# An LSTM with a residual: first loads, first products and the activation table rearranged

## The chip, the cores and the metric

The kernel runs on one core of a Trainium2 chip. A time is the device time of one execution in microseconds (us); where several are given, their median counts. A profile describes one execution; its span runs from the first to the last instruction. The engines are named as the profile names them: PE (TensorE, with PEld for its weight loads), DVE (VectorE), ACT (ScalarE), POOL (GpSimd) and SP (SyncE, which issues all DMAs here).

## The reference, cut to what matters

x is 32 sequences of 512 steps with 512 features, in float32. One LSTM layer of width 512 runs over the steps, and its output is added to x:

```
xW = einsum('ntd,dg->ntg', x, Wx) + b          # Wx: 512 x 2048
a = xW[:, t] + h @ Wh                          # Wh: 512 x 2048
i, f, o = sigmoid(a[:, :3*512]);  g = tanh(a[:, 3*512:])
c = f * c + i * g;   h = o * tanh(c)
x + h of all steps
```

The products with Wx are free of the recurrence; those with Wh are not: step t+1 needs h of step t.

## The kernel before, in words

Four gates of 512 values for 32 sequences are held as a tile of 128 partitions (4 blocks j of 32 sequences' rows) by 4 gates by 128, exactly one PSUM bank. TensorE is used as four column strips of 32: every product is issued for j = 0 to 3 in turn, each j writes 32 partitions of the bank, and the profile shows each product as two MATMUL records (128 x 32 weights loaded by PEld, then 128 or 512 moving columns).

Per step t there are three kinds of work.

- `h_part(t)`: 16 products of 512 columns, h of step t-1 times Wh (L427 in the profile). They add to the bank `gates_of(t)`: `ge` for even t, `go[0]` and `go[1]` in turn for odd t.
- `cell(t)`: ACT's sigmoids and tanh, DVE's products and the two transposes that give `ht`, which the next `h_part` waits for (L440 to L459). The residual add is POOL's, the output DMA SP's.
- The products with Wx. For four steps together (a "quad") they are made by a two-level Strassen-Winograd scheme: sums of x (`early_sums`, `late_sums`), sums of weights (`outer_weight`, `inner_weight`, made once by DVE) and 128-column products (`inner`, L314) whose results are combined over several steps. It has a pipeline 11 steps long (`LEAD`). So the first eight steps and the last eight, for which it has no room, are made by plain products: `direct` (L341) multiplies a chunk of x by the raw Wx blocks. For one step, `direct` with `ALL` goes over four pairs (k, gg), each with e, g and j: 64 products of 128 columns, one gate each.

The order of the work is written out by hand in the loop over k at the end (`manual_schedule`): window k holds `h_part(k - 11)`, `evacuate(k)`, the biases of `bias_at`, sums, `make_weights(k)`, `input_part(k)`, the plain products of `direct_at` and `cell(k - 11)`. Every engine executes its part of that list in order. The start is windows 8, 9 and 10, where there is no `h_part` yet: there the plain products of steps 0, 1 and 3 are made as pieces of Wx arrive, four pairs over three windows; those of step 2 (whose bank `ge` is still in use by step 0) come in window 12 behind `input_part`, followed by steps 5, 4, 7 and 6 in windows 13 to 16. A bank is emptied by `clear` (products of zeros with `start`, 16 of 128 columns) and given the bias by `set_bias`, an ACT copy.

All loads are issued on SP in program order: x chunks 0 and 1 (8 steps each, 512 KB), the bias, h0, four loads of Wx of 1 MB, four of Wh of 1 MB. They use eight DMA semaphores in turn, so a load is issued only when the load eight places ahead of it has landed. The Wx blocks lie in `w_sb[1]`, `w12`, `w_sb[2]` and `w_sb[3]`, slots 0 to 3 of each; in the host's layout the four blocks have the order (e, g) = (0,0), (1,0), (1,1), (0,1). In the tail, one block of each of two tiles has been overwritten by then and is loaded again by `reload` at window 505 (256 KB each).

Of the kernel before, what the change touches and what calls it, by code (L numbers as in the profile page):

```python
# [20 lines left out]
LAST = T // 4 - 2  # L21
# [7 lines left out]
def kernel(  # L29
# [59 lines left out]
    def gates_of(t):  # L89
        if t >= 4 * LAST:  # L90
            return last_banks[t - 4 * LAST]
        return ge if t % 2 == 0 else go[(t % 4) // 2]


    xcs, sums = {}, {}

    def load_chunk(c):
        xc = xpool.tile([P, TC, NJ, B], F32, name=f"xc_{c}", tag="xc")
        nc.sync.dma_start(out=xc.rearrange("p t q b -> p (t q b)"), in_=x[c])
        xcs[c] = xc  # L100
# [67 lines left out]

    load_chunk(0)
    load_chunk(1)
    bias_sb = const.tile([P, G, P], F32, name="bias_sb")
    for j in range(NJ):
        nc.sync.dma_start(
            out=bias_sb[j * B : (j + 1) * B, :, :],
            in_=bias[j].unsqueeze(0).to_broadcast([B, G, P]),
        )
    h_init = const.tile([P, NJ, B], F32, name="h_init")  # L180
    nc.sync.dma_start(out=h_init.rearrange("p q b -> p (q b)"), in_=h0)
    w_sb = {r: const.tile([P, 8 if r == 1 else 7, NJ, P], F32, name=f"w_{r}") for r in range(1, 8)}
    w12 = const.tile([P, 4, NJ, P], F32, name="w12")
    raw = {(0, 0): w_sb[1], (0, 1): w12, (1, 0): w_sb[2], (1, 1): w_sb[3]}
    for i in ((0, 0), (0, 1), (1, 0), (1, 1)):
        nc.sync.dma_start(out=raw[i][:, 0:4].rearrange("p s j u -> p (s j u)"), in_=wx[2 * i[0] + i[1]])
    wh_sb = const.tile([P, NJ, NJ, G * P], F32, name="wh_sb")
    for k in range(NJ):
        nc.sync.dma_start(out=wh_sb[:, k], in_=wh[:, k])

    def outer_weight(r):
        a, b = {5: (w12, w_sb[1]), 7: (w_sb[3], w12), 6: (w_sb[3], w_sb[5]), 4: (w_sb[2], w_sb[6])}[r]
        nc.vector.tensor_sub(w_sb[r][:, 0:4], a[:, 0:4], b[:, 0:4])

    def inner_weight(r, s):
        w = w_sb[r]
        a, b = {5: (3, 0), 6: (2, 4), 7: (2, 3), 4: (1, 5)}[s]
        nc.vector.tensor_sub(w[:, place(r, s)], w[:, a], w[:, b])

    def place(r, s):  # L200
        return 7 if (r, s) == (1, 4) else s - 1

    def raw_block(k, gg, e, g, late):
        n = {(0, 0): 0, (1, 0): 1, (1, 1): 2, (0, 1): 3}[e, g]
        if late and k == 1 and n == 3:
            return w_sb[5][:, 4 + gg]
        return raw[k, gg][:, n]

    def reload():

        for gg in range(2):
            nc.sync.dma_start(
                out=w_sb[5][:, 4 + gg].rearrange("p j u -> p (j u)"),
                in_=wx[2 + gg][:, 3 * NJ * P : 4 * NJ * P],
            )


# [2 lines left out]
    zero = const.tile([P, P], F32, name="zero")  # L220
# [5 lines left out]

    def clear(bank):

        for n in range(4):
            for j in range(NJ):  # L230
                nc.tensor.matmul(
                    bank[j * B : (j + 1) * B, n],
                    zero[:, 0:B],
                    zero,
                    start=n == 0,
                    stop=True,
                    skip_group_check=True,
                )

    U = {}  # L240

    def start_sums():
        nc.vector.tensor_sub(db, bias_sb[:, 2:4], b1)
        nc.vector.memset(xr1, 0.0)
        nc.vector.tensor_copy(xr1[:, 2], b1[:, 0])
        nc.vector.tensor_copy(xr5[:, 2], db[:, 0])
# [84 lines left out]
        for s in ss:  # L331
            inner(r, s, quad, dst[s])

    def direct(t, pairs):

        c, tt = divmod(t, TC)
        for k, gg in pairs:
            for e in range(2):
                for g in range(2):
                    for j in range(NJ):  # L340
                        nc.tensor.matmul(  # L341
                            gates_of(t)[j * B : (j + 1) * B, 2 * gg + g],
                            xcs[c][:, tt, 2 * k + e],
                            raw_block(k, gg, e, g, t >= 4 * LAST)[:, j],
                            start=False,
                            stop=True,
                            skip_group_check=True,
                        )

    def set_bias(t):  # L350
        nc.scalar.copy(gates_of(t), bias_sb)

    def quad_at(r, k, stage):

# [140 lines left out]
    def make_weights(k):  # L495
        for what in weights.get(k - 4 * FIRST, ()):
            outer_weight(what) if isinstance(what, int) else inner_weight(*what)


    ALL = ((0, 0), (0, 1), (1, 0), (1, 1))  # L500
    bias_at = {12: (2,), 13: (5,), 14: (4,), 15: (7,), 16: (6,)}
    direct_at = {
        8: [(t, ALL[0:1]) for t in (0, 1, 3)] + [(t, ALL[1:2]) for t in (0, 1, 3)],
        9: [(t, ALL[2:3]) for t in (0, 1, 3)],
        10: [(t, ALL[3:4]) for t in (0, 1, 3)],
        **{k: [(t[0], ALL)] for k, t in bias_at.items()},
    }
    end = 4 * LAST
    free_at = (510, 511, 510, 511, 513, 513, 514, 515)
    todo = [(end + i, (pair,)) for i in range(8) for pair in ALL]  # L510
# [13 lines left out]
    assert not todo  # L524

    with tc.manual_schedule():
        for bank in (ge, *go, pp):
            clear(bank)
        for t in (0, 1, 3):
            set_bias(t)  # L530
        for op in early_sums(nc.gpsimd, 1):
            op()
        start_sums()
        make_weights(4 * FIRST - 1)
        early, late = {}, {}
        for k in range(4 * FIRST, WINDOWS):
            t = k - LEAD
            c, rest = divmod(k + 5, TC)
            if rest == 0 and 2 <= c < NCHUNK:
                load_chunk(c)  # L540
            if k == 4 * LAST + 1:
                reload()
            if t >= 0:
                h_part(t)
            evacuate(k)
            for i in bias_at.get(k, ()):
                if gates_of(i) in (pb, *pa):
                    clear(gates_of(i))
                set_bias(i)
            for first, make, made, cut in ((-1, early_sums, early, 5), (3, late_sums, late, 3)):  # L550
                c, rest = divmod(k - first, TC)
                if (2 if make is early_sums else 1) <= c < NCHUNK - 1 and rest in (0, 2):
                    if rest == 0:
                        made[c] = make(nc.vector, c)
                    for op in made[c][:cut] if rest == 0 else made.pop(c)[cut:]:
                        op()
            make_weights(k)
            if t < 0:
                for what in direct_at.get(k, ()):
                    direct(*what)  # L560
            input_part(k)
            if t >= 0:
                for what in direct_at.get(k, ()):
                    direct(*what)
                cell(t)
# [5 lines left out]
def _laid_out(name, a):  # L571

    import numpy as _np

    if name == "x":
        a = a.reshape(B, NCHUNK, TC, NJ, NJ, B).transpose(1, 3, 5, 2, 4, 0).reshape(NCHUNK, P, TC * P)
    elif name == "cond_1024":
        a = a.reshape(B, NJ, NJ, B).transpose(1, 3, 2, 0).reshape(P, P)
    elif name == "L0_cond_Wx":

        a = a.reshape(NJ, 2, 2, B, 2, 2, NJ, P).transpose(1, 4, 0, 3, 2, 5, 6, 7).reshape(4, P, 4, NJ * P)
        a = a[:, :, [0, 2, 3, 1]].reshape(4, P, 4 * NJ * P)
    elif name == "L0_cond_Wh":
        a = a.reshape(NJ, NJ, B, G, NJ, P).transpose(0, 2, 1, 4, 3, 5).reshape(P, NJ, NJ, G * P)
    else:
        a = a.reshape(G, NJ, P).transpose(1, 0, 2)
    return _np.ascontiguousarray(a)
# [22 lines left out]
```

## Time and profile before

| what | value |
|---|---|
| median of three runs | 3177.79 us (3177.13 to 3181.36) |
| the profiled execution's own time | 3177.66 us |
| its span | 3175.6 us |
| PE busy | 3153.6 us, 99% |
| DVE, ACT, POOL busy | 70%, 40%, 8% |
| PE idle, 6.50 to 11.36 us | 4.86 us |
| PE idle, 19.32 to 20.72 and 24.41 to 26.90 us | 1.40 and 2.48 us |
| first `h_part` starts | 29.3 us |
| second `h_part` starts | 36.54 us |

The profile has a page and answers on parts of it. The chain of work lists, in order of time, what the last instruction was waiting for, step by step back to the start; "issue" in it is time for which the profile shows no cause. The timeline lists groups of instructions with start, duration, engine, line, written and read tiles, their shape and count, and in brackets the engine's idle time before them with what ended it. The windows view gives each engine's busy time in chosen stretches. In the DMA view q1 is the queue of the kernel's loads and stores and q8 a queue of instruction blocks.

### The profile page before, as it was taken

What the parts mean: (1) busy time and instruction counts of PE and PEld (TensorE: products, weight loads), DVE (VectorE), ACT (ScalarE), POOL (GpSimd) and SP (SyncE); (2) the same over time, 40 slices, a digit from 0 to 9 for tenths busy, and PEclk for the clock granted to TensorE, in tenths of its full rate; (3) what the DMA queues carried; (4) which work ended last, traced back from release to release, by engine and by line L of the source; (5) the groups of instructions that cost most, each with busy time, mean ns of one, the idle gap of its engine ahead of it and who ended that gap; (6) DMA issues with size and microseconds to landing.
All of it is one profiled execution on the core that took longest, in us unless ns stands there. A gap on an engine that the chain in (4) does not pass through costs nothing.

```text
span 3175.6 us, 151795 instructions
## 1 busy us (share of the span) xinstructions
PE 3153.6 (99%) x67296; PEld 1925.2 (61%) x67296; DVE 2232.2 (70%) x9226; ACT 1277.5 (40%) x4190; POOL 241.8 (8%) x525
## 2 busy tenths in 40 slices
PE   8999999999999999999999999999999999999999
PEld 6666666666666666666666666666666666666655
DVE  6777777777777777777777777777777777777762
ACT  2343444344434444444444444444444444444432
POOL 0000000000000000000000000000000000000000
PEclk9999999999999999999999999999999999999999
DMA  3000000000000000000000000000000000000000
GB/s 137 26 20 28 26 21 26 28 20 28 20 28 26 21 26 28 20 28 20 28 26 21 27 28 20 28 20 28 26 21 26 28 20 28 20 28 26 21 26 14
DMA packets 48659, 86.07 MB, mean 27 GB/s; under 512 B 5376, under 2 KB 38400, under 8 KB 46976
## 3 DMA queue, kind: packets, MB, share of 16 engines
q1 hardware_dynamic: 48000, 76.37, 7.5%
q8 instruction: 525, 8.60, 1.1%
q14 instruction: 134, 1.10, 0.1%
HBM read 42.80 MB, written 33.55 MB: 24 GB/s over the span
## 4 chain that ended last, share of the span: by engine, by line
PE 99%; DVE 1%; ACT 0%; DMA 0%; issue 0%; SPq 0%; DVEq 0%; ACTq 0%
PE go L427 27%; PE ge L427 27%; PE pa L314 18%; PE pp L314 10%; PE pb L314 6%; PE ge L314 5%; PE go L314 3%; PE go L341 1%; PE ge L341 1%; PE pa L427 0%; PE pa L341 0%; DMA w<-in_L_cond_Wx_dram 0%; PE pp L341 0%; ACT s L440 0%; PE pb L427 0%
## 5 line engine op out<-in xcount | busy, mean ns | idle before, releaser
L427 PE MATMUL go<-wh_sb,ht 128*32 128x512 f32 x8128 | 918.7, 592 | 5.9 <-DVE ht L459 5.8
L427 PE MATMUL ge<-wh_sb,ht 128*32 128x512 f32 x8064 | 911.4, 592 | 0.9 <-DVE ht L459 0.8
L449 DVE TENSOR_TENSOR fc<-s,c 128x128 f32<-128x128 f32 x511 | 149.5, 292 | 577.4 <-ACT s L440 577.4
L427 PEld LDWEIGHTS go<-wh_sb,ht 128*32 128x32 f32 x8128 | 255.4, 110 | 464.1 <-issue 454.7
L427 PEld LDWEIGHTS ge<-wh_sb,ht 128*32 128x32 f32 x8064 | 256.5, 110 | 454.0 <-issue 415.8
L470 POOL TENSOR_TENSOR oc<-xc,ht 128x128 f32<-128x128 f32 x511 | 237.2, 464 | 2919.3 <-issue 1467.9
L440 ACT ACTIVATE s<-ge 128x256 f32<-128x256 f32 x253 | 97.1, 384 | 823.1 <-PE ge L427 823.1
L314 PE MATMUL pa<-w,n 128*32 128x128 f32 x5952 | 299.2, 273 | 0.0
L455 ACT ACTIVATE ig<-c 128x64 f32<-128x64 f32 x1024 | 206.1, 248 | 220.9 <-DVE c L453 220.9
L440 ACT ACTIVATE s<-go 128x256 f32<-128x256 f32 x254 | 97.5, 384 | 439.9 <-PE go L427 439.9
L457 DVE TENSOR_TENSOR fc<-s,ig 128x64 f32<-128x64 f32 x1024 | 190.1, 226 | 97.3 <-ACT ig L455 97.3
L314 PEld LDWEIGHTS pa<-w,n 128*32 128x32 f32 x5952 | 180.9, 110 | 75.4 <-issue 38.6
L314 PEld LDWEIGHTS pa<-w,na 128*32 128x32 f32 x3968 | 124.3, 110 | 148.6 <-issue 110.4
L258 ACT COPY u<-pp 128x512 f32<-128x512 f32 x248 | 145.4, 586 | 141.4 <-PE pp L314 141.4
L314 PE MATMUL pa<-w,na 128*32 128x128 f32 x3968 | 199.6, 273 | 0.0
L314 PE MATMUL pa<-w,nb 128*32 128x128 f32 x3968 | 199.3, 273 | 0.0
L314 PE MATMUL pp<-w,sa 128*32 128x128 f32 x3968 | 199.3, 273 | 0.0
L459 DVE STREAM_TRANSPOSE ht<-fc 128x64 f32<-128x64 f32 x1024 | 190.6, 224 | 1.5 <-DVE fc L457 0.9
L451 DVE TENSOR_TENSOR ig<-s 128x64 f32<-128x64 f32 x1024 | 181.3, 219 | 0.0
L453 DVE TENSOR_TENSOR c<-fc,ig 128x64 f32<-128x64 f32 x1024 | 181.2, 219 | 0.0
L314 PEld LDWEIGHTS pa<-w,nb 128*32 128x32 f32 x3968 | 121.2, 110 | 74.2 <-issue 38.0
L369 DVE TENSOR_TENSOR p<-u,p 128x512 f32<-128x512 f32 x124 | 86.0, 694 | 113.9 <-ACT u L258 113.9
(148 smaller groups left out, 5326.6 us busy)
## 6 DMA issues: line engine op xcount, KB each, us to landing
xc<-in_x_dram SPq DMA_DIRECT2D x64, 512.0 KB, 3.9
out_dram<-oc SPq DMA_DIRECT2D x255, 128.0 KB, 2.0
w<-in_L_cond_Wx_dram SPq DMA_DIRECT2D x4, 1024.0 KB, 9.5
wh_sb<-in_L_cond_Wh_dram SPq DMA_DIRECT2D x4, 1024.0 KB, 17.1
w<-in_L_cond_Wx_dram SPq DMA_DIRECT2D x2, 256.0 KB, 4.1
bias_sb<-in_L_cond_b_dram SPq DMA_DIRECT2D x4, 64.0 KB, 4.6
h_init<-in_cond_dram SPq DMA_DIRECT2D x1, 64.0 KB, 4.0
out_dram<-oc SPq DMA_DIRECT2D x1, 64.0 KB, 1.6
```

Of the source, the lines that this page charges most:

```text
L258: nc.scalar.copy(u, pp)
L314: nc.tensor.matmul(dst[j * B : (j + 1) * B], operand(r, s, quad), w_sb[r][:, place(r, s), j], start=start, stop=True, skip_group_check=True,)
L369: nc.vector.tensor_add(U["p5", q], U[4, q], U["p5", q])
L427: nc.tensor.matmul(g[j * B : (j + 1) * B], state["ht"][:, k, :], wh_sb[:, k, j, :], start=False, stop=True, skip_group_check=True,)
L440: nc.scalar.activation(s[:, 0:2, :], g[:, 0:2, :], AF.Sigmoid)
L449: nc.vector.tensor_mul(fc, s[:, 1, :], state["c"])
L451: nc.vector.tensor_mul(ig[:, u], s[:, 0, u], s[:, 3, u])
L453: nc.vector.tensor_add(c[:, u], fc[:, u], ig[:, u])
L455: nc.scalar.activation(tc_t[:, u], c[:, u], AF.Tanh)
L457: nc.vector.tensor_mul(h[:, u], s[:, 2, u], tc_t[:, u])
L459: nc.vector.transpose(ht[:, 2 * i : 2 * i + 2].rearrange("p q b -> p (q b)"), h[:, u])
L470: nc.gpsimd.tensor_add(state["oc"][:, tt % 2], xcs[n][:, tt], ht)
```

## The change

- **Loads.** Chunk 0 of x comes in two halves; only the first (steps 0 to 3) is loaded first, the second after Wh. The bias is second. Each Wx load is split in two of 512 KB, in the order in which the products use them, and chunk 1 goes between the second and third pair of them. h0 goes after Wx.
- **Step 2.** In windows 8 to 10 the products of steps 2, 0 and 1 are made. Those of step 2 use the bank of step 3; when they are complete, `park` copies the bank (bias included) to SBUF, and `set_bias(2)` in window 12 copies it from there in place of the bias. Step 3's products follow: two pairs in window 10, one in window 11, one in window 12, the latter two behind `input_part`. Window 12 no longer has step 2's 64 products.
- **Width.** `direct` makes products of 256 columns (two gates), 32 for a step in place of 64. For that the Wx blocks lie in the order (e, g) = (0,0), (0,1), (1,0), (1,1), and the slots of sums (`place`, `inner_weight`) and the blocks reloaded in the tail follow (512 KB each).
- **Clear.** `clear` makes four products of 512 columns of zeros, in place of 16 of 128.
- **Table.** A sigmoid of the zero tile is ACT's first instruction. ACT then has one table load in the program, where it had one before its first copy and one before the first sigmoid.

```diff
+    load_first(0)
     for j in range(NJ):
         nc.sync.dma_start(out=bias_sb[j * B : (j + 1) * B, :, :], ...)
+    load_raw(0, 0)
+    load_raw(0, 1)
+    load_chunk(1)
+    load_raw(1, 0)
+    load_raw(1, 1)
     nc.sync.dma_start(out=h_init.rearrange("p q b -> p (q b)"), in_=h0)
-    for i in ((0, 0), (0, 1), (1, 0), (1, 1)):
-        nc.sync.dma_start(out=raw[i][:, 0:4].rearrange("p s j u -> p (s j u)"), in_=wx[2 * i[0] + i[1]])
     for k in range(NJ):
         nc.sync.dma_start(out=wh_sb[:, k], in_=wh[:, k])
+    load_first(1)
...
     def clear(bank):
-        for n in range(4):
-            for j in range(NJ):
-                nc.tensor.matmul(bank[j * B : (j + 1) * B, n], zero[:, 0:B], zero, start=n == 0, ...)
+        for j in range(NJ):
+            nc.tensor.matmul(
+                bank[j * B : (j + 1) * B], zero[:, 0:B],
+                zero.unsqueeze(1).to_broadcast([P, 4, P]), start=True, stop=True,
+            )
...
-    def direct(t, pairs):
+    def direct(t, pairs, bank=None):
         for k, gg in pairs:
             for e in range(2):
-                for g in range(2):
-                    for j in range(NJ):
-                        nc.tensor.matmul(
-                            gates_of(t)[j * B : (j + 1) * B, 2 * gg + g],
-                            xcs[c][:, tt, 2 * k + e],
-                            raw_block(k, gg, e, g, t >= 4 * LAST)[:, j], ...
+                for j in range(NJ):
+                    nc.tensor.matmul(
+                        bank[j * B : (j + 1) * B, 2 * gg : 2 * gg + 2],
+                        xcs[c][:, tt, 2 * k + e],
+                        raw_blocks(k, gg, e, t >= 4 * LAST)[:, :, j], ...
...
     def set_bias(t):
-        nc.scalar.copy(gates_of(t), bias_sb)
+        nc.scalar.copy(gates_of(t), parked.pop(t, bias_sb))
+    def park(t, bank):
+        parked[t] = upool.tile([P, 4, P], F32, name="parked", tag="u3")
+        nc.scalar.copy(parked[t], bank)
...
-    direct_at = {
-        8: [(t, ALL[0:1]) for t in (0, 1, 3)] + [(t, ALL[1:2]) for t in (0, 1, 3)],
-        9: [(t, ALL[2:3]) for t in (0, 1, 3)],
-        10: [(t, ALL[3:4]) for t in (0, 1, 3)],
-        **{k: [(t[0], ALL)] for k, t in bias_at.items()},
-    }
+    direct_at = {k: [(t, ALL) for t in bias_at[k] if t > 2] for k in bias_at}
+    direct_at[11], direct_at[12] = [(3, ALL[2:3])], [(3, ALL[3:4])]
+    def first_direct(k):
+        pairs = {8: ALL[0:2], 9: ALL[2:3], 10: ALL[3:4]}.get(k, ())
+        for pair in pairs:
+            direct(2, (pair,), gates_of(3))
+            if k == 10:
+                park(2, gates_of(3))
+                set_bias(3)
+            for t in (0, 1):
+                direct(t, (pair,))
+        if k == 10:
+            direct(3, ALL[0:2])
...
+        warm = work.tile([P, G, P], F32, name="warm", tag="s")
+        nc.scalar.activation(warm[:, 0], zero, AF.Sigmoid)
-        for bank in (ge, *go, pp):
+        for bank in (go[1], ge, go[0], pp):
             clear(bank)
-        for t in (0, 1, 3):
+        for t in (3, 0, 1):
             set_bias(t)
```

More of the change, by code (lines that the diff above doesn't have):

```diff
@@ L167, in operand, with load_first, load_raw @@
         return z["n" + group][:, SUM[s], 2 * i + d]
-    load_chunk(0)
-    load_chunk(1)
-    bias_sb = const.tile([P, G, P], F32, name="bias_sb")
+    xcs[0] = xpool.tile([P, TC, NJ, B], F32, name="xc_0", tag="xc")
+    def load_first(half):
+        n = TC // 2
+        nc.sync.dma_start(
+            out=xcs[0][:, half * n : (half + 1) * n].rearrange("p t q b -> p (t q b)"),
+            in_=x[0][:, half * n * P : (half + 1) * n * P],
+        )
+    bias_sb = const.tile([P, G, P], F32, name="bias_sb")
+    h_init = const.tile([P, NJ, B], F32, name="h_init")
+    w_sb = {r: const.tile([P, 8 if r == 1 else 7, NJ, P], F32, name=f"w_{r}") for r in range(1, 8)}
+    w12 = const.tile([P, 4, NJ, P], F32, name="w12")
+    raw = {(0, 0): w_sb[1], (0, 1): w12, (1, 0): w_sb[2], (1, 1): w_sb[3]}
+    wh_sb = const.tile([P, NJ, NJ, G * P], F32, name="wh_sb")
+    def load_raw(k, gg):
+        for e in range(2):
+            nc.sync.dma_start(
+                out=raw[k, gg][:, 2 * e : 2 * e + 2].rearrange("p s j u -> p (s j u)"),
+                in_=wx[2 * k + gg][:, 2 * e * NJ * P : 2 * (e + 1) * NJ * P],
+            )
+    load_first(0)
     for j in range(NJ):
@@ L179 @@
         )
-    h_init = const.tile([P, NJ, B], F32, name="h_init")
-    nc.sync.dma_start(out=h_init.rearrange("p q b -> p (q b)"), in_=h0)
-    w_sb = {r: const.tile([P, 8 if r == 1 else 7, NJ, P], F32, name=f"w_{r}") for r in range(1, 8)}
-    w12 = const.tile([P, 4, NJ, P], F32, name="w12")
-    raw = {(0, 0): w_sb[1], (0, 1): w12, (1, 0): w_sb[2], (1, 1): w_sb[3]}
-    for i in ((0, 0), (0, 1), (1, 0), (1, 1)):
-        nc.sync.dma_start(out=raw[i][:, 0:4].rearrange("p s j u -> p (s j u)"), in_=wx[2 * i[0] + i[1]])
-    wh_sb = const.tile([P, NJ, NJ, G * P], F32, name="wh_sb")
+    load_raw(0, 0)
[3 more added lines that the diff above has]
+    load_raw(1, 1)
+    nc.sync.dma_start(out=h_init.rearrange("p q b -> p (q b)"), in_=h0)
     for k in range(NJ):
         nc.sync.dma_start(out=wh_sb[:, k], in_=wh[:, k])
+    load_first(1)
     def outer_weight(r):
@@ L196, in inner_weight, with raw_blocks @@
         w = w_sb[r]
-        a, b = {5: (3, 0), 6: (2, 4), 7: (2, 3), 4: (1, 5)}[s]
+        a, b = {5: (1, 0), 6: (3, 4), 7: (3, 1), 4: (2, 5)}[s]
         nc.vector.tensor_sub(w[:, place(r, s)], w[:, a], w[:, b])
     def place(r, s):
[L201 to L207, printed above, removed]
+        return 7 if (r, s) == (1, 4) else {1: 0, 2: 2, 3: 3, 4: 1}.get(s, s - 1)
+    def raw_blocks(k, gg, e, late):
+        if late and k == 1 and e == 0:
+            return w_sb[5][:, 2 * gg : 2 * gg + 2]
+        return raw[k, gg][:, 2 * e : 2 * e + 2]
     def reload():
@@ L212, in reload @@
             nc.sync.dma_start(
-                out=w_sb[5][:, 4 + gg].rearrange("p j u -> p (j u)"),
-                in_=wx[2 + gg][:, 3 * NJ * P : 4 * NJ * P],
+                out=w_sb[5][:, 2 * gg : 2 * gg + 2].rearrange("p s j u -> p (s j u)"),
+                in_=wx[2 + gg][:, 0 : 2 * NJ * P],
             )
@@ L227, in clear @@
     def clear(bank):
-        for n in range(4):
-            for j in range(NJ):
-                nc.tensor.matmul(
[L232 to L238, printed above, removed]
+        for j in range(NJ):
+            nc.tensor.matmul(
+                bank[j * B : (j + 1) * B],
+                zero[:, 0:B],
+                zero.unsqueeze(1).to_broadcast([P, 4, P]),
+                start=True,
+                stop=True,
+            )
     U = {}
@@ L332, in private @@
             inner(r, s, quad, dst[s])
-    def direct(t, pairs):
+    def direct(t, pairs, bank=None):
         c, tt = divmod(t, TC)
+        bank = gates_of(t) if bank is None else bank
         for k, gg in pairs:
             for e in range(2):
-                for g in range(2):
-                    for j in range(NJ):
-                        nc.tensor.matmul(
-                            gates_of(t)[j * B : (j + 1) * B, 2 * gg + g],
-                            xcs[c][:, tt, 2 * k + e],
[L344 to L348, printed above, removed]
+                for j in range(NJ):
+                    nc.tensor.matmul(
+                        bank[j * B : (j + 1) * B, 2 * gg : 2 * gg + 2],
+                        xcs[c][:, tt, 2 * k + e],
+                        raw_blocks(k, gg, e, t >= 4 * LAST)[:, :, j],
+                        start=False,
+                        stop=True,
+                        skip_group_check=True,
+                    )
+    parked = {}
     def set_bias(t):
-        nc.scalar.copy(gates_of(t), bias_sb)
+        nc.scalar.copy(gates_of(t), parked.pop(t, bias_sb))
+    def park(t, bank):
+        parked[t] = upool.tile([P, 4, P], F32, name="parked", tag="u3")
+        nc.scalar.copy(parked[t], bank)
     def quad_at(r, k, stage):
@@ L558 @@
             if t < 0:
-                for what in direct_at.get(k, ()):
-                    direct(*what)
+                first_direct(k)
             input_part(k)
@@ L579, in _laid_out @@
     elif name == "L0_cond_Wx":
-        a = a.reshape(NJ, 2, 2, B, 2, 2, NJ, P).transpose(1, 4, 0, 3, 2, 5, 6, 7).reshape(4, P, 4, NJ * P)
-        a = a[:, :, [0, 2, 3, 1]].reshape(4, P, 4 * NJ * P)
+        a = a.reshape(NJ, 2, 2, B, 2, 2, NJ, P).transpose(1, 4, 0, 3, 2, 5, 6, 7).reshape(4, P, 4 * NJ * P)
     elif name == "L0_cond_Wh":
```

## The prediction

> **What bounds the kernel now.** I read the page first. PE is busy for 3153.6 of 3175.6 us; 22.0 us are idle. Whatever the change gains must be PE work taken away or PE idle time closed. The chain of waits in order of time shows where the idle time lies: at the start, before the second `h_part`.
>
> ```profile
> PE 3153.6 (99%) x67296; PEld 1925.2 (61%) x67296; DVE 2232.2 (70%) x9226; ACT 1277.5 (40%) x4190; POOL 241.8 (8%) x525
> ```
>
> Chain of waits, first 80 us (start, duration, what):
>
> ```profile
> 3.97 7.26 DMA w<-in_L_cond_Wx_dram
> ...
> 18.89 0.43 PE ge L341 x14
> 19.32 1.40 issue
> ...
> 23.94 0.48 PE ge L341 x18
> 24.41 2.48 issue
> ...
> 29.60 3.56 PE ge L427 x30
> ...
> 33.22 1.28 ACT L440
> 34.51 0.01 issue
> 34.52 0.39 ACT s L440
> ...
> 36.54 3.64 PE go L427 x32
> ...
> 41.49 3.49 PE ge L341 x128
> 44.98 3.43 PE ge L427 x32
> ```
>
> The chain is made of: the first Wx load (landed at 11.22), plain products with two holes called "issue", `h_part(0)`, then 1.28 us of a table load ahead of the first sigmoid, the cell, and `h_part(1)` at 36.54. PE is without a gap from there to the tail. So the quantities to predict are the starts of `h_part(1)` (36.54) and `h_part(2)` (44.98); from then on the whole run is shifted.
>
> The windows view over the loads (PE, PEld, DVE, ACT, POOL, granted clock, DMA share, GB/s), and the end of the answer on `wh_sb`:
>
> ```profile
> 20.00:25.00 5.00, 3.69 (x127) 3.43 (x127) 4.72 (x7) 0.31 (x1) 0.00 (x0) 1.00 1.02 423
> 25.00:30.00 5.00, 3.10 (x99) 2.96 (x102) 1.05 (x4) 0.06 (x1) 0.00 (x0) 1.00 0.59 241
> ```
> ```profile
> DMA to landing us min/median/max: 14.0/17.1/20.1
> ```
>
> DMA is saturated at 423 GB/s until the loads are through. The last Wh load was issued at 8.4 and took 20.1 us: it landed at 28.5. So `h_part(0)`, which started at 29.3, was hardly later than its own data allow. This is the bound that remains at the start when PE's holes are closed.
>
> **What the Trainium skill says.** "Runtime: NRT & Kernel Launch", section Instruction fetch mechanics: instructions come in blocks of 16 KiB, 256 of them, fetched by DMA while the block before is executed, mostly hidden. The holes fit this, but not "hidden": 350 and 476 products (two instructions each) precede them, one block apart, and the DMA view has one 16 KB packet of q8 just ahead of each hole's end (in 18 to 19 us and 24 to 25 us), queued among the loads. From the resumption at 20.72 to the next at 26.90 are 6.2 us, so under load a block of 128 products at 27 ns (3.5 us) outruns its successor. "TensorE: Matmul & The Clock Gate", section "Wait — 56ns, not 53.3ns?": about 2.5 ns per product beside the columns. "ScalarE: Activation LUTs", section What ACT_TABLE_LOAD costs: 1283 ns; the trace has 1.28 us.
>
> **The change, part by part.**
>
> *Width.* `h_part`: 32 records of 512 columns in 3.43 us, 107.2 ns each. A plain step: 128 of 128 columns in 3.49 us, 27.3 ns each. A line through both gives 0.208 ns a column plus 0.6 ns (times four strips, the skill's 2.5 ns), so 53.9 ns for 256 columns, which no run shows yet; 64 records make 3.45 us a step, 0.04 less; a quarter of a step 0.86. Steps 5, 4, 7, 6 and some seven of the tail's eight lie on PE's chain: 11 x 0.04 = 0.45 us. (From below: no gain, 0; from above 3.43/3.49 of it, 0.06 each, 0.7.) The other effect is on fetches: a block of 128 records lasts 6.9 us, over 6.2, so the holes go. Together with the smaller clears, 96 records fewer, the second block boundary comes inside window 10 instead of at 14 us.
>
> *Clear.* 32 records at 27.3 = 0.87 against 8 at 107.2 = 0.86 each: nothing. At the start it lies under the wait for loads, in the tail once on the chain (3114.38, 0.92 us); equal either way.
>
> *Loads.* Ahead of the end of Wh the second half of chunk 0 is gone: 256 KB at 423 GB/s, 0.62 us. Against it stand smaller packets: records of 4 KB take 159 ns and of 8 KB 313, so 4 MB in 4 KB packets cost 0.16 us more, and the first half comes in 2 KB packets, about 0.1. At the front SP issues one load per 0.46 us and 1.0 us passes to the first packet: x half, four biases, so the first Wx half flows from 3.04 + 1.0 = 4.05; what precedes it is through by about 4.1 to 4.4, so the queue hardly runs dry. The eight-deep semaphore ring doesn't bind: the load that waits longest, the last of Wh, waits for the fifth Wx half (about 12.5) and has its turn at about 23. So the last Wh load lands at 28.5 - 0.3 = 28.2; bounds 27.2 (no fetch packet, 1.1 us each, on a late engine) and 29.5 (two on one).
>
> Is PE there by then? First Wx half at about 6.3, second 7.5, then one per 1.25 us: w12 at 10.0, chunk 1 11.3, w2 13.8, w3 16.3. Window 8: products in step with the loads until about 11.8, plus 0.44 of `input_part`; window 9 until about 16.2 (w2, 3 x 0.86, 0.65); window 10: five quarters, 4.3, plus 0.44, until about 20.9. `park` and the second `set_bias(3)` (0.59 each on ACT) lie under the 1.7 us of steps 0 and 1; without that cover 1.2 us, still ahead of the loads. POOL's sums begin at 11.3 instead of 6.2 and last 4.7 us, needed from about 12: the same cover. Then `h_part(0)` waits for Wh piece by piece. Spare time before its last quarter: 28.2 - 20.9 - 2.6 = 4.7 us. So a hole of 2.5 us there costs nothing; this hides everything before.
>
> *Last quarter of h_part(0).* 28.2 + 0.14 (landing to first product, 11.22 to 11.36) + 0.86 + 0.2 drain = 29.4.
>
> *Table.* Sigmoid at 29.46 instead of 34.52, of which 1.28 is the table load; its new place is under the first loads (ACT idle until 7.38).
>
> *Cell(0)* takes 2.02 (34.52 to 36.54): `h_part(1)` at 31.5. PE meanwhile has `input_part` 1.31 and one quarter 0.86, from 29.2 to 31.4: it fits. Gain so far 36.54 - 31.5 = 5.05.
>
> *Step 2's 3.49 us leave window 12*, a quarter (0.86) comes in. PE then needs 3.43 + 1.31 + 0.86 = 5.60 from `h_part(1)` to `h_part(2)`, but another wait takes over. The DVE timeline of window 12:
>
> ```profile
> 37.81 2.28 DVE L193 TENSOR_TENSOR w<-w,w 128x2048 f32<-128x2048 f32 x1
> 40.13 0.69 DVE L198 TENSOR_TENSOR w<-w 128x512 f32<-128x512 f32 x1
> 40.74 0.28 DVE L449 TENSOR_TENSOR fc<-s,c 128x128 f32<-128x128 f32 x1
> ...
> 42.04 0.36 DVE L459 STREAM_TRANSPOSE ht<-fc 128x64 f32<-128x64 f32 x2
> ```
>
> The weight sums are queued ahead of `cell(1)` on DVE, and `ht(1)` is ready 5.75 us after `h_part(1)` began. So `h_part(2)` comes 5.80 after `h_part(1)`, not 8.44: gain 2.64, total 7.7, `h_part(2)` at 37.3. What is late next: window 13 has 5.2 us of DVE work ahead of `cell(2)`, so `ht(2)` comes about 6.8 after `h_part(2)`; PE has 3.43 + 0.87 + 3.45 = 7.75, so PE leads again.
>
> *The reload* is 512 KB larger in all, issued at window 505, needed from 510, some 30 us later: hidden.
>
> Sum: 7.7 + 0.45 = 8.15. Against the profiled execution's own time, 3177.66 (span plus 2.1 around it), this gives 3169.5; its own time is 0.13 below the median of the runs, so the same holds for that.
>
> **Rivals.** (a) *The start sheds less: 3171.8.* PE's clock halves while it waits. The skill's clock page (section What's actually happening) has half rate after an idle window of 3.4 us, and this trace agrees: granted clock 0.66 in 10 to 15 us, after the hole of 4.86. In the new wait PE has 0.9 us of work per 2.5 us of Wh; the thinnest window that stayed full here had 1.5 of 3.4 (25.0 to 28.4). If 0.9 is too little, the last quarter and window 11 run at half: about 0.6 + 1.1 = 1.7 to 2.3 us lost. The same result if Wh lands at 30. Against it: no window is wholly idle. (b) *It sheds more: 3168.3.* No fetch packet delays the last Wh load: 27.2, gain 9.3. Against it: PE must cross two blocks during the loads. (c) *The holes move instead of closing*, 3169.5 to 3172: a fetch hole of 2.5 us after the last Wh load, in window 11. Against it: by then only 0.8 MB of loads remain. (d) *Slower, 3191.* The 256-column products read two strips of 512 bytes 2 KB apart, while all before read one run; if each cost the second strip's 27 ns again (81 ns), a step takes 5.2 us, +1.7 x 13 = +22 against -8. It decides from 0.63 us a step, 64 ns a record. Against it: the 512-column and 128-column rows lie on one line. (e) *No effect*, if `h_part(0)` was bound by loads that end at the same time: then still 1.28, step 2's 2.64 and 0.45 go, 3173.3.
>
> **Chances.** Forecast 0.66; (b) 0.12; (a) 0.10; (c) 0.04; (e) 0.05; (d) 0.03. A measurement of this kernel tells about 0.2%, 6.4 us, from no change: faster means below 3171.4. The forecast and (b) are there, half of (c) too; (a), (e) and half of (c) are "same", and I add a little for drift between runs. The range reaches from under (b) to just past (a): 3167.3 to 3172.8.
>
> **What would show it.** Right: `h_part(0)` in four pieces with waits of about 1.6 us for Wh, its end near 29.4; one table load, before 3 us; `h_part(1)` near 31.5 and `h_part(2)` near 37.3, released by DVE; records of 256 columns 54 ns apart; no "issue" holes after 20 us. Wrong: granted clock 0.5 around 28 to 32 us; the last Wh landing after 29.5; PE gaps in windows 13 to 16, which would mean that DVE's backlog stays the bound.

## The result

The changed kernel takes 3171.98 us (median of 17 executions, 3171.37 to 3174.03). The kernel before, run beside it, takes 3177.79 (17 executions, 3174.51 to 3181.36). The ratio is 0.9982, with a 95% interval of 0.9975 to 0.9989: about 6 us faster. 3169.5 was predicted, with a range of 3167.3 to 3172.8. So direction and range were right, and the size was 2.5 us off. The profiled execution took 3171.43 us with a span of 3169.7, against 3177.66 and 3175.6 before: 6.2 us less in time, 5.9 in span.

The executions fall into two groups, which matters below: ten lie from 3171.4 to 3172.1, seven from 3172.6 to 3174.0, and those seven have a mean granted clock of 0.999, to three digits (of the ten, eight have 1.0 and two 0.999). The profiled execution is one of the ten.

From the page of the changed kernel, the busy times:

```profile
PE 3152.9 (99%) x66080; PEld 1897.3 (60%) x66080; DVE 2231.1 (70%) x9226; ACT 1277.0 (40%) x4192; POOL 246.4 (8%) x525
```

PE has 1216 records fewer and only 0.7 us less of work; the other 5.2 of the 5.9 us of span are PE's idle time. Where they went shows in the chain of waits of the first 80 us (start, duration, what; L451 is `h_part`, L358 `direct`, L464 the sigmoid, L212 `outer_weight`):

```profile
5.78 8.88 DMA w<-in_L_cond_Wx_dram
14.68 14.92 DMA wh_sb<-in_L_cond_Wh_dram
...
29.64 1.11 PE ge L451 x8
...
30.78 0.39 ACT s L464
...
34.07 2.29 DVE w L212
...
38.68 3.64 PE ge L451 x32
...
46.65 1.67 PE go L451 x13
```

The two "issue" holes and the table load have left the path. What stands there now are the loads themselves: the fifth Wx half, which had to land before SP could issue the last Wh load, and then that load, issued at 14.68 and landed at 29.60. Then follow the last quarter of `h_part(0)`, the sigmoid 0.03 us behind it, and, further on, DVE's weight sums ahead of `cell(1)`. PE's timeline shows `h_part(0)` in pieces, with what ended the idle time before each in brackets:

```profile
24.55 1.90 PE L451 MATMUL ge<-wh_sb,h_init 128*32 128x512 f32 x16
27.13 1.07 PE L451 MATMUL ge<-wh_sb,h_init 128*32 128x512 f32 x8 [0.68 <-DMA wh_sb<-in_L_cond_Wh_dram]
29.64 1.06 PE L451 MATMUL ge<-wh_sb,h_init 128*32 128x512 f32 x8 [1.45 <-DMA wh_sb<-in_L_cond_Wh_dram]
```

Before, all four quarters ran together from 29.3 to 33.16, behind the holes. Now only the last is left when Wh is complete, and `h_part(0)` ends at 30.75. `h_part(1)` starts at 32.80 (3.74 earlier than before), `h_part(2)` at 38.68 (6.30 earlier), `h_part(3)` at 46.65 (6.13 earlier).

### The profile page after: what moved, and what is told of

It is laid out like the page before. It is cut to its first block, busy times and chain, and to the rows that moved or that the text cites. A ratio compares the mean times of both kernels' runs of the same rounds, so it can differ in the third digit from the quotient of the medians.

```text
span 3169.7 us, 149374 instructions
## 1 busy us (share of the span) xinstructions
PE 3152.9 (99%) x66080; PEld 1897.3 (60%) x66080; DVE 2231.1 (70%) x9226; ACT 1277.0 (40%) x4192; POOL 246.4 (8%) x525
## 4 chain that ended last, share of the span: by engine, by line
PE 98%; DMA 1%; DVE 1%; ACT 0%; SPq 0%; issue 0%; DVEq 0%; ACTq 0%
PE ge L451 27%; PE go L451 27%; PE pa L331 18%; PE pp L331 10%; PE pb L331 6%; PE ge L331 5%; PE go L331 3%; DMA wh_sb<-in_L_cond_Wh_dram 0%; PE go L358 0%; PE ge L358 0%; PE pa L451 0%; DMA w<-in_L_cond_Wx_dram 0%; PE pa L358 0%; ACT s L464 0%; PE pp L358 0%
## 5 line engine op out<-in xcount | busy, mean ns | idle before, releaser
L451 PE MATMUL go<-wh_sb,ht 128*32 128x512 f32 x8128 | 918.9, 592 | 3.8 <-DVE ht L483 3.7
L451 PE MATMUL ge<-wh_sb,ht 128*32 128x512 f32 x8064 | 911.5, 592 | 1.4 <-DVE ht L483 1.3
L451 PEld LDWEIGHTS go<-wh_sb,ht 128*32 128x32 f32 x8128 | 256.8, 110 | 462.0 <-issue 453.8
L451 PEld LDWEIGHTS ge<-wh_sb,ht 128*32 128x32 f32 x8064 | 257.6, 110 | 454.9 <-issue 414.9
L464 ACT ACTIVATE s<-ge 128x256 f32<-128x256 f32 x253 | 96.9, 383 | 828.3 <-PE ge L451 824.6
L464 ACT ACTIVATE s<-go 128x256 f32<-128x256 f32 x254 | 97.3, 383 | 439.4 <-PE go L451 439.4
```

What stands on the lines that cost most here:

```text
L451: nc.tensor.matmul(g[j * B : (j + 1) * B], state["ht"][:, k, :], wh_sb[:, k, j, :], start=False, stop=True, skip_group_check=True,)
L464: nc.scalar.activation(s[:, 0:2, :], g[:, 0:2, :], AF.Sigmoid)
```

## The experiments

Three questions were open: why the last Wh load landed 1.4 us later than forecast, what the second group of executions is, and which part of the change brings the gain. All times are medians. They were run in three sessions, in which the kernel before took 3178.76 (the first four), 3178.25 (no early sigmoid, step 2 late, 128 columns, three remedies) and 3178.43 (the other four).

### The changed kernel again

No edit; it stands beside the next three.

> The changed kernel once more, as the mark for the three beside it. Theory 'clock': some executions have a stretch at half TensorE clock during the wait for Wh; the times then fall in two groups, near 3171.5 (mean granted clock 1.0) and near 3173.1 (0.999), and a profile of the second kind shows granted clock 0.5 for 3.4 us somewhere between 20 and 33 us. Rival 'clock is no cause': the clock stretch lies elsewhere (before 20 us, or in the tail) and the two groups come from the landing of the last Wh load. In either case the last Wh load lands at 29 to 30 us and the second h_part starts 1.6 us after the first sigmoid... that is at about 32.8 us.

3171.61 us (3171.22 to 3173.42, 10 executions; ratio 0.9979, 0.997 to 0.9988). Seven lie at 3171.2 to 3171.6, three at 3172.9 to 3173.4 with clock 0.999. In its profile the last Wh load landed at 29.80. So both the late landing and the two groups recur.

### Wx in whole loads

```diff
 def load_raw(k, gg):
-    for e in range(2):
-        nc.sync.dma_start(out=raw[k, gg][:, 2*e : 2*e+2]..., in_=wx[2*k + gg][:, 2*e*NJ*P : 2*(e+1)*NJ*P])
+    nc.sync.dma_start(out=raw[k, gg][:, 0:4]..., in_=wx[2*k + gg])
```

> The changed kernel, but each Wx block set is loaded by one DMA of 1 MB again (8 KB per partition), in the changed order. Theory 'small pieces': the last Wh load came 1.4 us later than forecast because the Wx halves are moved in packets of 4 KB out of rows of 8 KB, which ran slow at every new Wx region. Then the last Wh load lands at 28.2 to 28.6 here, the second h_part starts at 31.5 to 31.9 and the time falls by about 1.2 us to some 3170.8. Rival 'cold start': the loss is in the first reads after the bias, when the queue has run empty, whatever the packet size; then it lands at 29.3 to 29.8 as in the changed kernel and the time stays.

3169.35 us (3169.22 to 3171.08, 6 executions; 0.9971, 0.996 to 0.9983). The last Wh load landed at 28.15, the forecast's 28.2, and five of six executions lie at 3169.2 to 3169.7, the forecast's 3169.5. The sixth, at 3171.08, is the one that was profiled, and it shows what the other group is. Two lines of its windows view (stretch, its length, busy time and records of PE, PEld, DVE, ACT and POOL, granted clock, DMA share, GB/s), and two of its chain (L447 is `h_part`):

```profile
25.00:28.39 3.39, 1.37 (x16) 0.32 (x16) 0.67 (x2) 0.00 (x0) 0.00 (x0) 1.00 0.89 354
28.39:31.80 3.41, 3.41 (x48) 2.27 (x44) 1.16 (x8) 1.12 (x5) 0.00 (x0) 0.50 0.06 23
```
```profile
10.80 17.34 DMA wh_sb<-in_L_cond_Wh_dram
...
28.19 1.80 PE ge L447 x8
```

While PE waits for Wh it is busy 1.37 of 3.39 us; then the clock is 0.50 for 3.41 us. The last quarter takes 1.80 in place of 1.11 us, and the products that follow it are late too: `h_part(1)` starts at 32.92 although Wh was there 1.45 us sooner than in the changed kernel. That is rival (a) of the prediction, with its price: 3171.08 less the 3169.3 of the others is 1.8 us.

The time fell by 2.3 us against the changed kernel beside it, where 1.2 had been expected. In the two profiles the landing accounts for 1.65 (29.80 less 28.15); no profile shows where the rest is.

### Halves, but contiguous in memory

The host lays each half out as a block of its own; the loads still move 512 KB in pieces of 4 KB per partition, in the same order.

```diff
-    in_=wx[2 * k + gg][:, 2 * e * NJ * P : 2 * (e + 1) * NJ * P],
+    in_=wx[2 * k + gg, e],
```

> The changed kernel with the Wx halves laid out in DRAM so that each half is one run of 512 KB; the packets stay 4 KB per partition. Theory 'small pieces' has two forms. If the packet size itself costs, nothing changes: last Wh landing at 29.3 to 29.8. If it is the stride (4 KB taken out of every 8 KB), it lands at 28.2 to 28.6 and the time falls by about 1.2 us. 'Cold start': no change.

3171.07 us (3169.92 to 3172.06, 8 executions; 0.9974, 0.9964 to 0.9985), in two groups: four at 3169.9 to 3170.35 with clock 1.0, four at 3171.8 to 3172.1 with clock 0.999 (the profiled one is of these: clock 0.5 from 28.64 to 32.05). The last Wh load landed at 28.44. The lower group lies 1.2 us under that of the changed kernel beside it (3171.2 to 3171.6), with pieces of the same size, so most of the lateness is not the size of the pieces but that 4 KB are taken out of every 8 KB. The 1.0 us down to the lower group of whole loads remains. The DMA view over the first 32 us gives the rate in slices of 0.8 us; first the changed kernel, then this one:

```profile
GB/s 0 0 195 277 174 149 195 282 374 405 364 353 420 405 415 364 394 420 364 302 374 414 431 430 399 440 451 410 430 399 430 430 420 415 379 397 282 105 41 0
```
```profile
GB/s 0 0 215 251 185 97 287 420 425 420 420 425 420 415 410 410 410 405 415 415 430 395 435 420 410 461 369 451 399 410 420 410 412 394 402 184 51 31 0 0
```

Both start slowly (149 and 97 GB/s in the sixth slice). With contiguous halves the rate is 420 from the eighth slice on; with strided halves it creeps up from 195 to 405 over four slices. So the loss lies at the start: the first Wx half landed at 8.33 in the changed kernel and at 6.88 here, and from there to the last Wh load it is 21.27 us in the one and 21.56 in the other. The later dip to 302 near 15 us costs nothing by this comparison. The rival of a cold start had the place right, but not that the layout makes no difference. This is one profile of each; six profiles with strided halves have the first half at 7.3 to 8.4 and the last Wh load at 29.3 to 30.1.

### PE kept busy during the wait

Four products of 512 columns of zeros, into a bank not in use then, ahead of the third and fourth quarter of `h_part(0)`.

```diff
         for k in range(NJ):
+            if t == 0 and k >= 2:
+                clear(pa[2])
```

> The changed kernel with four products of 512 columns of zeros into an unused bank (0.86 us of PE time) ahead of the third and of the fourth quarter of the first h_part, where PE waits for Wh anyway. Theory 'clock': with PE busy there, no stretch at half clock; all executions have granted clock 1.0 and lie near 3171.5, 0.5 us below the median of the changed kernel. Rival: the two groups remain, and the median is that of the changed kernel or up to 0.2 us more.

3171.62 us (3170.90 to 3172.11, 9 executions; 0.9978, 0.9967 to 0.9988). The upper group is gone: none of 9 above 3172.2, where the changed kernel has 10 of 27 above 3172.6. If their share were still 10 in 27, nine executions without one would come about once in sixty times (an estimate from these counts). Against the expectation, two of the nine (3170.90 and 3171.91) have a mean clock of 0.999, as two of the changed kernel's lower group have; the experiment after this one shows how that can be. The stretch that was thin with whole loads is full in this profile:

```profile
25.00:28.39 3.39, 3.39 (x36) 0.81 (x28) 1.62 (x5) 0.00 (x0) 0.00 (x0) 1.00 1.01 412
```

The median against the changed kernel of the same session (3171.61) is the same, since there only three of ten were in the upper group. The last Wh load landed at 29.27, so the loads' lateness is untouched: two separate causes.

### Without the early sigmoid

```diff
-        warm = work.tile([P, G, P], F32, name="warm", tag="s")
-        nc.scalar.activation(warm[:, 0], zero, AF.Sigmoid)
```

> The changed kernel without the sigmoid at ACT's start, so that the table for the sigmoids is loaded behind the first h_part again. Theory: the load of 1.28 us is wholly on the path there; the second h_part starts 1.3 us later after the end of the first, and the time is 1.3 us above the changed kernel's (about 3172.9 in the undisturbed group). Rival: PE has 2.2 us of other work there (input_part and a quarter of step 3), so that only a part shows, 0 to 0.5 us.

3171.79 us (3171.22 to 3173.98, 19 executions, five of them above 3172.4; 0.9981, 0.9974 to 0.9988): no difference from the changed kernel. A loss of 1.3 us had been expected, so this was a miss. ACT's timeline, before (first fence) and here:

```profile
33.22 1.28 ACT L440 ACT_TABLE_LOAD   x1 [8.16 <-PE ge L427]
```
```profile
23.80 0.37 ACT L306 COPY pp<-xr 128x256 f32<-128x256 f32 x1
24.18 1.28 ACT L464 ACT_TABLE_LOAD   x1
30.79 0.38 ACT L464 ACTIVATE s<-ge 128x256 f32<-128x256 f32 x1 [5.33 <-PE ge L451]
```

In the kernel before, the table load itself waited for PE: the wait for `h_part(0)` stood on it, and the sigmoid came 1.30 us later. Here the wait stands on the sigmoid; the load goes right behind ACT's previous copy, 6.6 us ahead of its use, under the wait for Wh. So other parts of the change had already taken the load off the path.

This profiled execution is of the lower group (3171.47) and has a stretch at half clock all the same:

```profile
13.69:17.11 3.42, 1.58 (x34) 0.60 (x28) 3.39 (x7) 0.00 (x0) 3.26 (x6) 1.00 1.02 410
17.11:20.52 3.41, 3.41 (x36) 1.74 (x33) 2.36 (x3) 0.00 (x0) 3.25 (x5) 0.50 1.04 430
```

PE was slow there, but still waited 0.67 us for the last Wh load afterwards. A half-clock stretch ahead of that wait cost nothing; those behind it went with the upper groups. So a mean clock of 0.999 does not by itself mark the upper group.

### Step 2 in window 12 again

```diff
-    direct_at = {k: [(t, ALL) for t in bias_at[k] if t > 2] for k in bias_at}
-    direct_at[11], direct_at[12] = [(3, ALL[2:3])], [(3, ALL[3:4])]
+    direct_at = {k: [(t, ALL) for t in bias_at[k]] for k in bias_at}
 ...
-            direct(2, (pair,), gates_of(3))
-            ...
-            for t in (0, 1):
+            for t in (3, 0, 1):
                 direct(t, (pair,))
-        if k == 10:
-            direct(3, ALL[0:2])
```

> The changed kernel with the plain products of step 2 in window 12 again (256 columns), those of steps 3, 0 and 1 in windows 8 to 10, nothing parked. Theory: from the second to the third h_part PE then needs 3.6 + 1.3 + 3.45 = 8.4 us in place of the 5.9 that DVE sets in the changed kernel, and nothing is won earlier because the first h_part waits for Wh: 2.5 us slower, about 3174.0. Rival: with one quarter less in windows 10 to 12 the first h_part ends earlier and takes back more than 0.5 us.

3173.96 us (3173.60 to 3175.73, 12 executions; 0.9986, 0.9977 to 0.9995), 2.2 more than the kernel of the experiment above, run beside it. From its chain:

```profile
33.16 3.64 PE go L451 x32
...
38.11 3.45 PE ge L358 x64
41.56 3.43 PE ge L451 x32
```

`h_part(2)` follows `h_part(1)` after 8.40 us, with step 2's 3.45 us directly between. In the changed kernel it is 5.88. The difference, 2.52, is close to what the prediction gave to this part (2.64).

### 128-column products in the changed kernel

```diff
             for e in range(2):
-                for j in range(NJ):
-                    nc.tensor.matmul(bank[j*B:(j+1)*B, 2*gg : 2*gg+2], ..., raw_blocks(...)[:, :, j], ...)
+                for g in range(2):
+                    for j in range(NJ):
+                        nc.tensor.matmul(bank[j*B:(j+1)*B, 2*gg + g], ..., raw_blocks(...)[:, g, j], ...)
```

> The changed kernel with products of 128 columns in direct, twice as many; all else as changed. Theory: the fetch holes come back (idle of PE put down to issue between 12 and 25 us, 1 to 2.5 us each), but lie ahead of the wait for the last Wh load; what shows is 11 x 0.04 = 0.45 us, and up to 1 us if another instruction block delays an engine of the load: 3171.9 to 3172.9 undisturbed. Rival: the holes push the last quarter of the first h_part beyond the landing of Wh, 2 us or more slower.

3175.51 us (3173.95 to 3177.24, 12 executions; 0.9993, 0.9985 to 1.0002): 3.7 more than the kernel without the early sigmoid beside it, where 0.45 to 1 had been thought likeliest. From the chain of its profiled execution (which was the 3177.24; L452 is `h_part`):

```profile
14.35 2.66 issue
...
26.84 2.21 issue
...
31.50 4.62 PE ge L452 x30
```

The "issue" holes are back, with one more of 0.96 at 22.07: 5.8 us in all. `h_part(0)` begins at 31.1, after the last Wh load (landed at 30.09), and all of it is on the path. Each hole ends 1.3 to 1.4 us after a 16 KB packet of q8 was through (15.63, 21.73 and 27.65). In this execution the clock was also 0.5 from 16.44 to 19.85 and from 30.09 to 33.50, so not all of its lateness is the holes. But the five executions at mean clock 1.0 have a median of 3174.6, and those of the kernel beside it at 1.0 one of 3171.7: without any half clock the narrow products still cost 2.9 us.

### 256 columns alone, in the kernel before

The kernel before with the wide `direct` and `clear` and the block order that they need; loads, step 2 and table as they were. The diff is the width part of the change.

> The kernel before with products of 256 columns (and the clears of 512 columns) alone: old loads, step 2 in window 12, the table load before the first sigmoid. Theory: the holes of 1.40 and 2.48 us go, because a block of instructions lasts longer than its successor takes to come; the last quarter of the first h_part then waits for Wh (28.5), ends at 29.7, and with the table load behind it the second h_part starts at 33.1 in place of 36.5; with 0.5 us for the columns, 3.9 us faster than before, about 3174.3. Rival: the width is worth its columns alone, 0.6 us (3177.6).

3173.87 us (3172.92 to 3175.73, 20 executions; 0.9988, 0.9981 to 0.9995): 4.6 less than before. From its chain (L448 is `h_part`, L461 the sigmoid with its table load):

```profile
8.60 19.66 DMA wh_sb<-in_L_cond_Wh_dram
...
28.30 1.11 PE ge L448 x8
...
29.48 1.28 ACT L461
...
32.79 5.34 PE go L448 x32
```

No holes; the last Wh load lands at 28.26, `h_part(0)` ends at 29.4, and the table load is on the path. `h_part(1)` starts at 32.79 and ran 5.34 instead of 3.64 us, because the clock was 0.5 from 34.1 to 37.5 in this execution.

### The early sigmoid alone, in the kernel before

```diff
+        warm = work.tile([P, G, P], F32, name="warm", tag="s")
+        nc.scalar.activation(warm[:, 0], zero, AF.Sigmoid)
         for bank in (ge, *go, pp):
```

> The kernel before with the sigmoid of zeros at ACT's start alone. There the table load of the first sigmoid carries the wait for the first h_part itself, so that it can't run ahead as it did without the early sigmoid in the changed kernel. Theory: the first sigmoid follows the end of the first h_part by 0.06 us in place of 1.36, the second h_part starts 3.4 - 1.3 = 2.1 us after the end of the first, and the time falls by 1.3 us against the kernel before. Rival: PE's own work there, or a clock stretch, hides it: under 0.5 us.

3177.28 us (3174.71 to 3178.32, 12 executions; 0.9996, 0.9988 to 1.0005): 1.15 less by medians, which the interval doesn't tell from nothing. The profile does show the step: `h_part(0)` ends at 34.6, the sigmoid starts at 34.69, and `h_part(1)` follows 2.1 us after the end, where it was 3.4. `h_part(1)` still started at 36.70, no earlier than before, since the clock was 0.5 from 10.2 to 17.0 and from 27.2 to 30.7 in this execution.

### The changed kernel with the old loads

```diff
-    load_first(0)
+    nc.sync.dma_start(out=xcs[0]..., in_=x[0])
+    load_chunk(1)
     (bias)
-    load_raw(0, 0); load_raw(0, 1); load_chunk(1); load_raw(1, 0); load_raw(1, 1)
     (h0)
+    for i in ((0, 0), (0, 1), (1, 0), (1, 1)):
+        nc.sync.dma_start(out=raw[i][:, 0:4]..., in_=wx[2 * i[0] + i[1]])
     (Wh)
-    load_first(1)
```

> The changed kernel with the loads of the kernel before: both x chunks whole and first, bias, h0, four loads of Wx and four of Wh of 1 MB each. Theory: only the landing of the last Wh load counts, and the earlier start of the plain products is hidden; it lands near 28.5 to 28.9, with PE ready for the last quarter of the first h_part by about 27.5, so the second h_part starts at 31.7 to 32.1 and the time is that of the changed kernel or 1 to 1.5 us less, 3169.8 to 3171.5. Rival 'the order is what gains': PE starts its products at 11.3 in place of 8.5 us, the first h_part ends 2 us later, 3173.5 or more.

3170.14 us (3169.19 to 3171.74, 15 executions; 0.9976, 0.9968 to 0.9983): seven at 3169.2 to 3169.5, eight at 3170.1 to 3171.7. The changed kernel has no execution of 27 under 3171.2. In the profile, of the upper group (3171.04), the last Wh load landed at 28.25 and the clock was 0.5 from 28.58 to 32.00. So the new order with its halves brought no gain; it cost 1.5 to 1.8 us by medians, and 2.1 between the lower groups (3171.5 less 3169.4). The two kernels were not run in the same session.

### Three remedies together

Whole Wx loads, the zeros of `keep_warm`, and DVE's sums for `w_sb[4]` one window earlier, ahead of `cell(0)`.

```diff
-        3: [(6, 7)],
-        4: [4, (6, 4)],
+        3: [(6, 7), 4, (6, 4)],
```

> Three edits on the changed kernel together: Wx in four loads of 1 MB, the products of zeros that keep PE busy ahead of the last two quarters of the first h_part, and the sums for w_sb[4] made by DVE in window 11 (ahead of cell(0), where it waits) in place of window 12. Theory: last Wh landing near 28.2, no stretch at half clock, the second h_part near 31.4 and the third 5.7 to 5.8 us later, released by PE's own order or the cell and no longer by DVE's sums: all executions between 3168.9 and 3169.6. Rival: a group 1.7 us above remains, or the third h_part comes 5.9 us after the second as before.

3169.69 us (3169.46 to 3170.52, 10 executions; 0.9974, 0.9965 to 0.9984), in one group, all at clock 1.0. The last Wh load landed at 29.13 in the profiled execution (the slowest of the ten), and `h_part(2)` came 5.82 after `h_part(1)`: released by PE's own work, no longer by DVE, and no sooner. Seven of the ten are above the expected 3169.6. That whole loads too can end at 29.13 shows that the start varies by itself: here the first MB of Wx landed at 8.95, in `whole_wx` at 8.30.

### A shorter start

Whole Wx loads, the first of them directly behind the first half of x; the bias as four rows of 2 KB, spread over the partitions by a product; the same move of DVE's sums; no zeros.

```diff
     load_first(0)
-    for j in range(NJ):
-        nc.sync.dma_start(out=bias_sb[j*B:(j+1)*B], in_=bias[j].unsqueeze(0).to_broadcast([B, G, P]))
     load_raw(0, 0)
+    for j in range(NJ):
+        nc.sync.dma_start(out=braw[j * B : j * B + 1], in_=bias[j].unsqueeze(0))
     load_raw(0, 1)
 ...
+        nc.tensor.matmul(pp, pick, braw, start=True, stop=True)
+        nc.scalar.copy(bias_sb, pp)
```

> An attempt at a faster one: the changed kernel with Wx in loads of 1 MB, the first of them issued right behind the half of x; the bias fetched as four rows of 2 KB behind it and spread over the partitions by one product with a matrix of ones in PSUM, in place of 256 KB; the sums for w_sb[4] in window 11. No products of zeros. Theory: the Wx stream starts at about 2.2 in place of 4.1 us and everything behind it comes 1.5 to 1.9 us earlier: last Wh landing 26.3 to 27.3, second h_part at 29.6 to 30.5, 3167.6 to 3168.4, since PE then hardly waits also without a group at half clock. Rival: PE is the bound by then (it reaches the last quarter at 26 to 27 us only), or the stretch at half clock comes back: 3169 to 3170.5.

3168.63 us (3168.39 to 3169.88, 8 executions, all at clock 1.0; 0.9971, 0.9961 to 0.9982): the fastest version here; its slowest execution is faster than the changed kernel's fastest. It still misses the expected 3167.6 to 3168.4. The last Wh load landed at 27.37, and PE waited only 0.2 us for it. The chain then runs over DVE (L211 and L216 are the weight sums, L450 `h_part`):

```profile
27.27 2.21 DVE w L211
29.51 0.69 DVE w L216
...
31.71 3.64 PE go L450 x32
```

The sums for `w_sb[4]`, moved ahead of `cell(0)`, now hold it: `h_part(1)` starts 4.3 us after the landing, against 3.2 in the changed kernel. With loads this early they are in the wrong place, which neither the theory nor the rival had.

## Why the prediction was right, and where it was not

**The sum.** By its own steps, in the profiled execution:

| step | predicted | measured |
|---|---|---|
| first Wx half has landed | 6.3 | 8.33 |
| last Wh load has landed | 28.2 | 29.60 |
| from there to `h_part(1)` | 3.3 | 3.20 |
| `h_part(1)` to `h_part(2)` | 5.80, set by DVE | 5.88, set by DVE |
| `h_part(2)` to `h_part(3)` | 7.75, set by PE | 7.97 |
| a record of 256 columns | 53.9 ns | 3.45 us / 64 = 53.9 ns |
| gain in all | 8.15 | 6.2 |

The step that was mis-sized is "Loads". 1.4 us of the missing 1.9 is there at `h_part(2)`, nearly all of it the late landing. Another 0.2 comes because `h_part(2)` starts on an idle PE (3.64 in place of 3.43 us), and 0.3 because PE waits 0.46 us for DVE in window 18, where it waited 0.12 before. A last landing after 29.5 was one of the prediction's own signs of being wrong, and the median lies nearest to rival (a)'s 3171.8, which it gives also for a landing at 30. The range holds the result because it was drawn to just past (a). (Two slips in its working change nothing: the gain of 9.3 given to rival (b) is 0.15 too large by its own terms, 8.15 plus 1.0, and the 350 and 476 "products" ahead of the holes are records.)

**Loads: the bound was right, the size was not.** Not in the sum for 28.2 was the slow start: the first Wx half was 2.0 us late, and from there to the last Wh load it is 21.3 us, where the forecast had 21.9. So all of the lateness arises before the first half has landed. The stride makes it worse: contiguous halves landed at 6.88 and end at 28.44, whole rows at 28.15 to 28.5 in four profiles (the kernel before is one) and at 29.13 in a fifth. What makes the first slices slow was not isolated. The bias's broadcast loads fall there, and the version without them landed at 27.37, but that version changed more than the bias.

**Rival (a) is true in part of the executions.** It had a chance of 0.10 as an alternative to the forecast; it comes and goes from one execution to the next. The Trainium skill's page "TensorE: Matmul & The Clock Gate", section What's actually happening, names an idle window of about 3.4 us and says that the window is free-running. The length agrees (3.41 us at 0.50), and a free-running window fits groups of executions of one program. That the window must be idle does not agree: 1.37 us of work in 3.39 us (40%) was followed by half rate. The traces allow more. In a trace the half-clock stretches start whole multiples of 3.413 us apart, so the windows between them can be counted off. In the fourteen profiles, up to 46 us after the start, PE was busy for at most 1.58 us in every window that half rate followed (3.413 us long; 2.12 in one that was itself at half rate), and for at least 1.53 in every other, leaving out the window in which the program starts. So for this kernel the border lies near 1.55 of 3.41 us, 45%. Where the windows fall decides the rest: in the changed kernel's two profiles the wait for the last Wh load falls into the window from 26.92 to 30.33 with 1.75 us of work and into that from 28.36 to 31.78 with 1.97, both above the border.

In the changed kernel itself no profile caught the half clock. Its upper group is put down to it by the size of the step (1.6 us between the groups' medians), because all profiled executions of upper groups of its variants with other loads show it (whole, contiguous and old), and because zeros in the wait remove the group.

**Width was credited with the wrong amount.** The prediction gave it 0.45 us on PE's chain. It did say that the holes go, but also that a hole of 2.5 us ahead of `h_part(0)` costs nothing, for the spare time of 4.7 us was to hide "everything before". Alone width is worth 4.6 us, and its absence in the changed kernel costs 3.7. The spare time was mis-sized too: `h_part(0)` began at 24.55, not at 20.9, and PE's waits for Wh are 2.1 us in all. The first Wx half was late, and POOL's sums, given 4.7 us from 11.3 on, ran from 13.45 to 23.25. The holes of narrow products, 5.8 us in all, exceed either figure. So width is most of the gain, and not through its columns. The Trainium skill, "Runtime: NRT & Kernel Launch", section Instruction fetch mechanics, has the next block fetched while the current one is executed. With the loads in flight that was not enough for 128-column products, which use up a block in half the time: the q8 packets just ahead of the holes fit this, and the same packets come in the changed kernel (through at 15.68 and 24.19) without a hole. That the fetch is the cause is argued from this; no run varied the fetch alone.

**Table: right number, wrong cause.** The sigmoid does follow `h_part(0)` at once. But without the early sigmoid it does too, since the load then runs under the wait for Wh. The 1.28 us are on the path in the kernel before and with width alone. Which of the other parts frees the load, step 2's move or the loads, was not tried.

**Step 2 was right,** mechanism and size: 2.52 between `h_part(1)` and `h_part(2)`, 2.2 in the medians.

**The parts add up otherwise than thought.** Width 4.6, then step 2 with the table 3.7 (3173.87 to 3170.14), then the new loads -1.5 to -2.1. Rival (e), in which closing the holes brings nothing, is excluded by the width alone; (b) by the landing at 29.60; (c) and (d) by the absence of holes and the 53.9 ns.

## What to carry to other kernels

Where a saturated load sets the start, work out what lands last before moving anything, and try whole rows: here, splitting a load across its rows to get the first piece sooner made the last one later. Count instructions as well as columns where instruction blocks queue behind loads; here, halving their number was worth ten times what it saves on the engine. A wait that left TensorE thinly busy cost again after its end, in some executions only, so look at all of them and not at the one that was profiled.

## What was not expected of the hardware

- A stretch of 3.39 us in which PE was 40% busy was followed by 3.41 us at half clock. Over all profiles the border lies near 1.55 us of work in a window of 3.41 (the fullest window with half clock behind it had 1.58, the emptiest without it 1.53).
- Reading 4 KB out of every 8 KB cost about 1.2 us (29.60 against 28.44 us), although each piece was of the same size, and all of it before the first 512 KB had landed.
- A table load with no wait of its own runs ahead of the activation that needs it: 6.6 us ahead in the kernel without the early sigmoid.
- POOL's sums took longer while DVE made a weight sum: one of 128x64 took 1.18 us in place of 0.32, one of 128x128 took 2.39 in place of 0.45, and each ended 0.2 to 0.3 us after DVE's. PE waited 0.8 us for another, which took 0.78, hidden under the loads.
